# Pairwise bilinear products: output stores of one size and a ring buffer without gaps

## Chip, cores, metric

One core of one Trainium2 chip. The metric is the device time of one execution in microseconds (us).

## The reference, cut to what matters

```python
# inputs: (4096, 32, 64) float32; W: (496, 64, 64) float32, one matrix for each pair of fields i < j
vi = inputs[:, i_idx, :]
vj = inputs[:, j_idx, :]
vdotw = jnp.einsum('bpd,pde->bpe', vi, W)
inter = vdotw * vj
return inter.reshape(B, -1)          # (4096, 31744) float32: 520 MB
```

A little is read (42 MB) and much is written (520 MB). The kernel works in 32 batch tiles of 128 rows; one tile makes 31,744 output columns on each of 128 partitions.

## The kernel before

PE (the matmul engine) multiplies field i (transposed) by its weights into PSUM (its result memory), DVE (the vector engine) multiplies the PSUM result by field j and writes the product into a ring in SBUF (the core's main on-chip memory), and the queue of SyncE stores pieces of the ring. Fields are handled in pairs (2p and 2p+1), whose outputs are `width[2p]` and `width[2p+1]` columns wide.

```python
STORES = [[0, 1], [2, 3], [4, 5], [6, 7, 8], [9, 10, 11, 12, 13, 14, 15]]   # field pairs of a store
RING = 28160
...
    store_w = [sum(width[2 * p] + width[2 * p + 1] for p in g) for g in STORES]
    # 7552, 6528, 5504, 6336, 5824 columns
...
    ring = const.tile([P, RING], F32, tag="ring", name="ring")
    at = 0
...
    for t in range(NT):
        ...                                        # load x of the next tile
        for s, group in enumerate(STORES):
            if at + store_w[s] > RING:
                at = 0                             # the rest of the ring stays empty
            osb = ring[:, at : at + store_w[s]]
            at += store_w[s]
            o0 = off[2 * group[0]]
            for p in group:
                ...                                # transposes for the next tile
                for c0 in range(0, width[2 * p], BANK):
                    ...                            # two matmuls into pm, one for each field
                    if n[0] == n[1]:
                        nc.vector.tensor_tensor(   # both fields in one instruction
                            runs(osb, o[0], o[1], n[0]), pm[:, :, : n[0]],
                            runs(xt, xj[0], xj[1], n[0]), ALU.mult)
                    else:
                        ...                        # one instruction for each field
            nc.sync.dma_start(out=out[ts(t, P), o0 : o0 + store_w[s]], in_=osb)
```

## Time and profile before

| | before |
|---|---|
| time, median | 1341.14 us (1341.14 to 1341.35, 3 runs) |
| span of the profiled run | 1339.7 us |
| PE, DVE, ACT busy | 86%, 88%, 5% |
| DMA queues together, share of 16 engines | 98.8% |
| transfers to the output | 160, 2752 to 3776 KB |

Busy shares of the engines are averages. Here the resource to watch is DMA: 16 engines work in parallel on every transfer, and a transfer counts as landed only when each has done its share: every transfer of this trace ends with 16 semaphore packets. "Share of 16 engines" says how long packets were under way, divided by 16 times the span. The issue lines of the page add how long a store is under way (columns: what, issuer, count, KB, median us from issue to landing), and its queue lines have packets, MB, share:

```profile
out_dram<-ring SPq DMA_DIRECT2D x32, 3776.0 KB, 22.8
...
out_dram<-ring SPq DMA_DIRECT2D x32, 2752.0 KB, 22.1
...
q14 instruction: 23, 0.19, 0.0%
```

The largest and the smallest store take the same 22 us, although a queue at 420 GB/s moves 3776 KB in 9.2 us: each waits behind one or two others. q8 and q14 carry the instructions themselves, fetched in blocks of 16 KiB (q8) and 8 KiB (q14). The main lines follow in the prediction, each with its reading.

### The profile page before, as it was taken

Reading aid. Unit: us, or ns where it says so; the run is one execution under the profiler, and the core shown is the slowest. Engines: PE = TensorE matmul, PEld = TensorE weight load, DVE = VectorE, ACT = ScalarE, POOL = GpSimd, SP = SyncE. Lnnn points to the kernel's source line nnn. Section 1 sums busy time; section 2 is a strip of 40 time slices with the busy share of each in tenths; the row PEclk is TensorE's granted clock in tenths of the full one; section 3 lists DMA queues with packets and bytes.
Section 4 is the critical chain, followed back from the end, with each engine's and each line's share of the span. In section 5 each row is a group of like instructions: output and inputs, shape, how many; then the busy total and the mean of one; then the engine's idle time right before and its main releaser. Section 6 shows DMA issues by size and latency. Waiting matters only on the chain.

```text
span 1339.7 us, 13755 instructions
## 1 busy us (share of the span) xinstructions
PE 1151.0 (86%) x5376; PEld 548.7 (41%) x5376; DVE 1177.4 (88%) x1664; ACT 66.1 (5%) x65; POOL 0.7 (0%) x6
## 2 busy tenths in 40 slices
PE   7998889888898888988888978889798897888992
PEld 3444344443343443443433534444344443444441
DVE  6999889888899988989888989899898997898993
ACT  1000000000000000000000000000000000000000
POOL 0000000000000000000000000000000000000000
PEclk9999889999999999989999899899898998998996
DMA  9999999999999999999999999999999999999996
GB/s 392 426 431 434 429 431 429 427 427 434 426 434 430 422 422 430 422 424 429 415 426 424 426 426 404 415 420 431 428 420 408 431 427 431 416 424 420 422 429 264
DMA packets 30017, 562.93 MB, mean 420 GB/s; under 512 B 3456, under 2 KB 3840, under 8 KB 5376
## 3 DMA queue, kind: packets, MB, share of 16 engines
q1 hardware_dynamic: 25344, 528.49, 92.6%
q10 hardware_dynamic: 4608, 33.56, 6.0%
q8 instruction: 42, 0.69, 0.2%
q14 instruction: 23, 0.19, 0.0%
HBM read 41.94 MB, written 520.09 MB: 420 GB/s over the span
## 4 chain that ended last, share of the span: by engine, by line
DMA 54%; DVE 23%; PE 11%; issue 9%; DVEq 0%
DMA out_dram<-ring 54%; DVE ring L130 15%; PE pm L120 9%; DVE ring L139 9%; PE pt L80 2%; DMA x<-in_x_dram 1%; DVEq L130 0%; DVEq L177 0%
## 5 line engine op out<-in xcount | busy, mean ns | idle before, releaser
L120 PE MATMUL pm<-w,xT 64*128 64x512 f32 (+7 forms) x4864 | 1083.2, 559 | 158.3 <-DVE ring L130 140.1
L130 DVE TENSOR_TENSOR ring<-pm,x 128x1024 f32<-128x1024 f32 x768 | 904.0, 1217 | 138.4 <-DMA out_dram<-ring 93.0
L120 PEld LDWEIGHTS pm<-w,xT 64*128 64x128 f32 x4864 | 487.7, 194 | 720.1 <-DVE ring L130 451.3
L139 DVE TENSOR_TENSOR ring<-pm,x 128x448 f32<-128x448 f32 (+6 forms) x896 | 330.2, 415 | 3.6 <-PE pm L120 2.9
L81 ACT COPY xT<-pt 128x1024 f32<-128x1024 f32 x64 | 64.8, 1012 | 1194.6 <-PE pt L80 1194.6
L80 PE MATMUL pt<-ident,x 128*128 128x128 f32 x512 | 76.5, 297 | 8.5 <-DMA x<-in_x_dram 8.5
L80 PEld LDWEIGHTS pt<-ident,x 128*128 128x128 f32 x512 | 61.0, 152 | 48.9 <-issue 35.3
L81 ACT ACT_TABLE_LOAD x1 | 1.3, 1283 | 1.7 <-PEq L173 1.7
masks.py:199 POOL TENSOR_SCALAR_AFFINE_SELECT ident<-ident 128x128 f32<-128x128 f32 x1 | 0.3, 292 | 0.1
masks.py:197 POOL MEMSET ident<- 128x128 f32 x1 | 0.2, 204 | 0.3 <-POOLq L173 0.3
L173 POOL MEMSET const-bfloat16-1.0<- 128x1 bf16 x1 | 0.1, 101 | 0.0
L173 POOL MEMSET const-uint8-127<- 128x1 uint8 x1 | 0.1, 101 | 0.0
L173 POOL MEMSET const-float32-0.0<- 128x1 f32 x1 | 0.1, 98 | 0.2 <-issue 0.2
L173 POOL MEMSET const-float32-1.0<- 128x1 f32 x1 | 0.1, 98 | 0.0
## 6 DMA issues: line engine op xcount, KB each, us to landing
out_dram<-ring SPq DMA_DIRECT2D x32, 3776.0 KB, 22.8
out_dram<-ring SPq DMA_DIRECT2D x32, 3264.0 KB, 21.8
out_dram<-ring SPq DMA_DIRECT2D x32, 3168.0 KB, 22.4
out_dram<-ring SPq DMA_DIRECT2D x32, 2912.0 KB, 22.3
out_dram<-ring SPq DMA_DIRECT2D x32, 2752.0 KB, 22.1
x<-in_x_dram ACTq DMA_DIRECT2D x32, 1024.0 KB, 14.2
w<-in_w_dram SPq DMA_DIRECT2D x1, 992.0 KB, 7.4
w<-in_w_dram SPq DMA_DIRECT2D x1, 928.0 KB, 11.7
```

The source lines that it names most:

```text
L80: nc.tensor.transpose(pt[:, ts(c, P)], xt[:, ts(n * g + c, P)], ident)
L81: nc.scalar.copy(xT[:, ts(g, 2 * BANK)], pt)
L120: nc.tensor.matmul(pm[:, h, : n[h]], xT[h * D : (h + 1) * D, ts(p, P)], w_sb[p][h * D : (h + 1) * D, c0 : c0 + n[h]], start=True, stop=True,)
L130: nc.vector.tensor_tensor(runs(osb, o[0], o[1], n[0]), pm[:, :, : n[0]], runs(xt, xj[0], xj[1], n[0]), ALU.mult,)
L139: nc.vector.tensor_tensor(osb[:, o[h] : o[h] + n[h]], pm[:, h, : n[h]], xt[:, xj[h] : xj[h] + n[h]], ALU.mult,)
L173: nc = bacc.Bacc("TRN2", target_bir_lowering=False, num_devices=1)
```

## The change

The intent: stores of one size (eight of 3968 columns a tile) instead of five unequal ones, and a ring of exactly seven of them in which nothing stays empty, so that more output is in flight and places come free in smaller pieces. Products are now placed by their output column modulo the ring, without regard to pairs; a product that meets the ring's end is cut.

```diff
-STORES = [[0, 1], [2, 3], [4, 5], [6, 7, 8], [9, 10, 11, 12, 13, 14, 15]]
-RING = 28160
+STORE_W = 3968
+RING = 7 * STORE_W
...
-        for s, group in enumerate(STORES):
-            if at + store_w[s] > RING:
-                at = 0
+        g0 = t * sum(width)
+        sent = 0
+        for p in range(NPR):
...
+                at = [(g0 + o[h]) % RING for h in range(2)]
-                    if n[0] == n[1]:
+                if n[0] == n[1] and at[0] < at[1] <= RING - n[1]:
                     ...                                    # one instruction for both fields
+                else:                                      # pieces, cut at the ring's end
                     for h in range(2):
+                        k = 0
+                        while k < n[h]:
+                            a = (at[h] + k) % RING
+                            m = min(n[h] - k, RING - a)
                             ...
+                            k += m
-            nc.sync.dma_start(out=out[ts(t, P), o0 : o0 + store_w[s]], in_=osb)
+                done = o[0] + n[0] if c0 + n[0] < width[2 * p] else o[1] + n[1]
+                while sent + STORE_W <= done:
+                    a = (g0 + sent) % RING
+                    nc.sync.dma_start(
+                        out=out[ts(t, P), sent : sent + STORE_W], in_=ring[:, a : a + STORE_W])
+                    sent += STORE_W
```

## The prediction

> **What bounds the kernel now.** I read the page's slices and queues first, to see which resource is full.
>
> ```profile
> DMA  9999999999999999999999999999999999999996
> GB/s 392 426 431 434 429 431 429 427 427 434 426 434 430 422 422 430 422 424 429 415 426 424 426 426 404 415 420 431 428 420 408 431 427 431 416 424 420 422 429 264
> ...
> q1 hardware_dynamic: 25344, 528.49, 92.6%
> q10 hardware_dynamic: 4608, 33.56, 6.0%
> q8 instruction: 42, 0.69, 0.2%
> ```
>
> The reader sees 16 DMA engines at 9 tenths or more in 39 of 40 slices; weights and stores (q1), loads of x (q10) and fetched instructions (q8) fill 98.8% of them. PE (86%) and DVE (88%) have room. Only the last slice is low, so I cut the end of the run into stretches (time, PE, weight loads, DVE, ACT, POOL, clock, DMA share, GB/s):
>
> ```profile
> 1233.00:1310.00 77.00, 69.84 (x318) 34.09 (x314) 70.49 (x101) 2.02 (x2) 0.00 (x0) 0.95 1.00 426
> 1310.00:1320.00 10.00, 6.21 (x28) 3.50 (x28) 9.26 (x18) 0.00 (x0) 0.00 (x0) 0.83 0.93 398
> 1320.00:1328.00 8.00, 0.00 (x0) 0.00 (x0) 0.00 (x0) 0.00 (x0) 0.00 (x0) 0.66 0.91 389
> 1328.00:1338.40 10.40, 0.00 (x0) 0.00 (x0) 0.00 (x0) 0.00 (x0) 0.00 (x0) 0.50 0.06 25
> ```
>
> The compute is over before 1320 us. From 1328 to 1338.4 us the share is 0.06, one sixteenth: **one DMA engine works on alone for 10.4 us after the other 15 have finished.** I call it the late engine. The packet records of the trace (start, duration, size) say where the delay comes from. Of the 128 row packets of a tile's first store, the last 8 (one engine's share) end after the other 120 by 1.6 us in tile 0, 2.2 us in tile 2, 6.9 us in tile 10, 10.0 us in tile 18, and then 8 to 11 us to the end. So one engine carries more than the others: every engine has the same rows, and the 42 fetches of 16,384 bytes on q8 are what differs. Which engine carries them the records do not name; that it is this one I infer from the sum below.
>
> From 1328 us to its end its packets follow each other without a gap. Is it ever idle earlier? It ends the first store of tile 2 at 119.4 us, of tile 17 at 736.1, of tile 18 at 777.1, of tile 31 at 1309.6: 41.1 us a tile in the first stretch, 41.0 in the second. It never slows down, although its lag stops growing. What changes is the other 15: from tile 18 on they run dry at times (slices 24, 29 and 30 at 404 to 420 GB/s), because a ring place comes free only when the late engine has read it. The waits of DVE and of the store queue:
>
> ```profile
> DVE ring L130 <- DMA out_dram<-ring: 93.0, 53, 3.3
> DVE ring L130 <- PE pm L120: 45.4, 52, 13.2
> ...
> SPq L145 <- DVE ring L139: 1228.7, 159, 10.5
> ```
>
> DVE waits 93 us in all for the ring, at most 3.3 us at once, while a store takes 22 us from issue to landing: two stores and more are always queued, so the late engine does not starve in these waits. The sum for it, from medians of the records: 8 rows of each of five stores (818+865+940+968+1119 ns) x 32 tiles = 1205.8 us; x, 8 rows x 309 ns x 32 = 79.1; the 16 weight loads 20.6; semaphore writes (9 ns each) 1.9; together 1307.4 us. It runs from about 2.8 to 1338.4 us, 1335.6 us, which leaves 28 us. 42 fetches at 611 ns (16,384 bytes at the line below) are 25.7 us. That nearly closes it. **The time is the late engine's own work from start to end, with about 2.8 us before and 1.3 us behind.**
>
> **What the Trainium skill says.** "DMA: Bandwidth & Descriptors", section "Specifications", gives a ceiling of 435 GB/s for the 16 engines, 27.2 a piece; the records agree, since a byte costs 0.0367 ns (27.2 GB/s). Its section "Why a DMA increments its semaphore by 16 and not by 1" says that each engine adds one and that only the full 16 means all data landed; that is why the slowest engine frees the ring, and the lag that levels off at 10 us agrees. "Runtime: NRT & Kernel Launch", section "Instruction fetch mechanics", says instructions come in blocks of 16 KiB, 256 each, over a DMA queue; PE has 5376 matmuls and 5376 weight loads, 10,752 in all, exactly 42 blocks, which is what q8 shows. "VectorE: DVE Perf Modes", section on the TRN2 errata, gives (N+151)/0.96 ns for a float32 tensor_tensor: 1224 ns for 1024 elements and 224 for 64, where the trace has 1217 and 215.
>
> **The change, part by part.**
> Bytes: stored and loaded bytes are the same. PE's instructions are the same, so q8 stays at 42 fetches.
> Packets: five rows per partition and tile become eight of 15,872 bytes. The medians of the records lie on a straight line, 9.1 ns + 0.03674 ns a byte (22,016: 818; 30,208: 1119; the three between within 1 ns), so a row should take 592 ns. Consecutive packets of one engine overlap in the records by 3 to 4 ns (in the tail, rows of 865 ns start every 861), so a row's real overhead is about 5.2 ns, a semaphore write's 6. Per engine and tile this adds 3x8 = 24 rows and 3 semaphore writes: 24x5.2 + 3x6 = 143 ns, x 32 = **4.6 us, all on the late engine's path**. With the recorded 9 ns uncut it would be 27 x 9 x 32 = 7.8 us. This is the whole direct cost.
> DVE: from the programs' order DVE has 1737 multiplies for 1664, 73 more: pairs cut at the ring's end or whose second row wraps. The shapes' rows give 148 ns fixed (64 columns 215 ns, 448 columns 617), so 73 x 148 = 10.8 us, 0.34 us a tile. DVE goes from 36.8 to 37.1 us busy a tile against 41 for the late engine: beside other work, worth nothing.
> Store issues: 256 for 160 at 0.33 us each on a queue that mostly waits: nothing. The eight DMA semaphores are reused after eight transfers and the ring holds seven stores, so that wait is over before it starts.
> Ring: before, places left empty at the end keep it at four to five stores in flight or being filled. After, it is 27,776 columns always in use and freed in pieces of 3968 (4.7 us of pure row time) rather than up to 7552. DVE's waits for the ring should fall from 93 us to some 40 to 80, and the 15 others should starve less and finish further ahead, the lag growing to perhaps 12 to 18 us. **That gains nothing: they do not set the end.** If anything the late engine loses a little: its 41.0 us a tile with others idle was 41.1 with them busy, about 1 to 2 us over 14 tiles.
> Start: the first store could go about 6 us earlier, but the store queue is still issuing weights up to 23.7 us (its first store left at 24.6), and the DMA share is already 1.0 from 4 us on. Nothing.
> End: a smaller last store shortens the part behind DVE's last write, but the late engine has some 20 us of queued work by then. Nothing.
> Sum: 1341.1 + 4.6 + 1 = about **1347 us**.
>
> **The rivals.**
> *The ring's gaps starve DMA, and filling them gains.* For it: slices at 404 to 420 GB/s and 93 us of DVE waits. If all 16 engines ran at the 430 GB/s of the early stretches, 562.9 MB would take 1309 us, and with start and end some 1315 to 1320, almost 2% less. Against: the lost share belongs to the 15 engines that are ahead; the late engine's pace does not change. A ring moves none of its work. I give it 6%.
> *Smaller packets cost more than the line says*, for instance where x rows or fetches interleave (rows beside x loads show extra time, on average 21 ns for the last store's rows). If every added row cost 25 ns, the sum would be 24x25x32 = 19 us, 1360 us. Against: rows of 6400 to 7424 bytes of the weights lie on the same line, and the extra time is counted twice, in two overlapping packets.
> *DVE becomes the bound, since split writes wait for places further ahead.* It would need 3.5 us more a tile; 0.3 are added. Waiting with five stores queued still leaves some 25 us of DMA work.
> *Rows at whole multiples of 512 bytes are faster* (two of the old stores start or end half-way). The line fits those stores' medians within 1 ns, so I expect nothing.
>
> **Range and chances.** The core of the estimate is 1346 to 1349 us (4.6 to 7.8 us). Packet costs a little worse or a fetch that now overlaps better widen it to 1341 to 1353 us, 8 times in 10. Over 2% faster would need under 1315 us, below what even the first rival makes likely; over 2% slower needs 1368 us, a packet overhead five times what is seen. Same is nearly certain.
>
> **What would show it.** Right: row packets of about 592 ns; q1 with 39,168 packets, 528.5 MB and a share that has hardly moved; q8 still 42; a tail at share 0.06 longer than 10.4 us; DVE's waits for the ring shorter and the middle slices nearer 430 GB/s, with the end no earlier. The late engine's pace should be about 41.2 to 41.3 us a tile. Wrong: a shorter tail with an earlier end (the late engine was held by the ring after all), or rows well above 592 ns.

## The result

| | before | after |
|---|---|---|
| time, median | 1341.24 us (1341.14 to 1341.47, 4 runs) | 1346.80 us (1346.57 to 1346.95, 4 runs) |
| span of the profiled run | 1339.7 us | 1344.9 us |
| DVE: instructions, busy | 1664, 1177.4 us | 1737, 1181.6 us |
| 15 engines finish, last engine finishes (packet records) | 1328.2, 1338.4 us | 1326.1, 1343.7 us |

The ratio is 1.0041 (95% interval 1.0024 to 1.0058), slower by 5.6 us. By the measure of 2% used here the two kernels count as the same; the 5.6 us are small but clear of the noise.

The slices and queues of the kernel after:

```profile
DMA  9999999999999999999999999999999999999994
GB/s 387 429 431 425 425 429 425 425 425 426 430 427 426 425 424 430 425 427 425 425 425 428 427 426 424 424 430 426 424 426 427 425 425 422 424 419 420 426 428 176
...
q1 hardware_dynamic: 39168, 528.50, 92.9%
q10 hardware_dynamic: 4608, 33.56, 5.9%
q8 instruction: 42, 0.69, 0.2%
q14 instruction: 25, 0.20, 0.0%
```

The dips to 404, 408 and 415 GB/s in the middle are gone, and between the first slice and the last none is under 419. A reader who stopped here would expect a faster kernel. But the last slice fell from 264 to 176. Its stretches (time, PE, weight loads, DVE, ACT, POOL, clock, DMA share, GB/s):

```profile
1310.00:1320.00 10.00, 4.06 (x26) 2.25 (x24) 6.84 (x15) 0.00 (x0) 0.00 (x0) 0.97 1.00 423
1320.00:1328.00 8.00, 0.00 (x0) 0.00 (x0) 0.00 (x0) 0.00 (x0) 0.00 (x0) 0.50 0.55 234
1328.00:1338.40 10.40, 0.00 (x0) 0.00 (x0) 0.00 (x0) 0.00 (x0) 0.00 (x0) 0.50 0.06 26
1338.40:1344.00 5.60, 0.00 (x0) 0.00 (x0) 0.00 (x0) 0.00 (x0) 0.00 (x0) 0.50 0.06 26
```

The 15 engines finished 2.0 us earlier than before, at 1326.1 us, and then one engine worked alone for 17.6 us instead of 10.3. What the deeper ring gave to the 15 did not reach the end. The waits of DVE:

```profile
DVE ring L124 <- DMA out_dram<-ring: 106.2, 74, 2.8
...
DVE ring L136 <- DMA out_dram<-ring: 9.8, 12, 2.3
```

Together DVE waits 116 us for ring places, where it waited 93. The landings of the tiles' last stores are 41.2 to 41.3 us apart in most tiles, where they were 41.0 to 41.2 before: the late engine keeps its pace, with a little more work.

### The profile page after: what moved, and what is told of

The parts are those of the page before. It is cut to its first block, busy times and chain, and to the rows that moved or that the text cites. A ratio compares the mean times of both kernels' runs of the same rounds, so it can differ in the third digit from the quotient of the medians.

```text
span 1344.9 us, 14075 instructions
## 1 busy us (share of the span) xinstructions
PE 1138.1 (85%) x5376; PEld 534.3 (40%) x5376; DVE 1181.6 (88%) x1737; ACT 66.1 (5%) x65; POOL 0.7 (0%) x6
## 3 DMA queue, kind: packets, MB, share of 16 engines
q1 hardware_dynamic: 39168, 528.50, 92.9%
q10 hardware_dynamic: 4608, 33.56, 5.9%
## 4 chain that ended last, share of the span: by engine, by line
DMA 66%; DVE 15%; PE 10%; issue 6%; DVEq 0%
DMA out_dram<-ring 66%; DVE ring L124 10%; PE pm L113 8%; DVE ring L136 5%; PE pt L78 2%; DMA x<-in_x_dram 1%; DVEq L124 0%; DVEq L182 0%
## 5 line engine op out<-in xcount | busy, mean ns | idle before, releaser
L124 DVE TENSOR_TENSOR ring<-pm,x 128x1024 f32<-128x1024 f32 x727 | 854.1, 1214 | 124.6 <-DMA out_dram<-ring 106.2
L113 PEld LDWEIGHTS pm<-w,xT 64*128 64x128 f32 x4864 | 477.9, 191 | 738.7 <-DVE ring L124 429.8
L136 DVE TENSOR_TENSOR ring<-pm,x 128x256 f32<-128x256 f32 (+7 forms) x1010 | 379.7, 425 | 10.6 <-DMA out_dram<-ring 9.8
L78 PE MATMUL pt<-ident,x 128*128 128x128 f32 x512 | 71.4, 284 | 8.6 <-DMA x<-in_x_dram 8.6
L78 PEld LDWEIGHTS pt<-ident,x 128*128 128x128 f32 x512 | 56.4, 143 | 42.1 <-issue 39.4
```

Source lines behind the costliest of these rows:

```text
L78: nc.tensor.transpose(pt[:, ts(c, P)], xt[:, ts(n * g + c, P)], ident)
L113: nc.tensor.matmul(pm[:, h, : n[h]], xT[h * D : (h + 1) * D, ts(p, P)], w_sb[p][h * D : (h + 1) * D, c0 : c0 + n[h]], start=True, stop=True,)
L124: nc.vector.tensor_tensor(runs(ring, at[0], at[1], n[0]), pm[:, :, : n[0]], runs(xt, xj[0], xj[1], n[0]), ALU.mult,)
L136: nc.vector.tensor_tensor(ring[:, a : a + m], pm[:, h, k : k + m], xt[:, xj[h] + k : xj[h] + k + m], ALU.mult,)
```

## The experiments

Ten kernels ran, each with five rounds (runs 3, 4 and 6 have four times); the runs of before beside them had medians of 1341.23 (runs 1 to 4), 1341.30 (5 to 8) and 1341.32 us (9 and 10). All results were correct. "Tail" is the time, from the packet records, between the second last engine's end and the last one's.

| run | time, us | against before | ratio, 95% interval | packets q1, blocks q14 and q8 | tail, us |
|---|---|---|---|---|---|
| before | 1341.24 | | | 25,344, 23, 42 | 10.3 |
| after | 1346.80 | +5.6 | 1.0024 to 1.0058 | 39,168, 25, 42 | 17.6 |
| 1 ring only | 1343.40 | +2.2 | 1.0003 to 1.0028 | 29,952, 24, 42 | 10.8 |
| 2 five places | 1346.65 | +5.4 | 1.0028 to 1.0053 | 39,168, 25, 42 | 9.1 |
| 3 sixteen stores | 1361.38 | +20.2 | 1.0134 to 1.0165 | 76,032, 29, 42 | 7.6 |
| 4 split rows | 1394.83 | +53.6 | 1.0385 to 1.0414 | 25,365, 23, 42 | 10.2 |
| 5 more PE code | 1418.46 | +77.2 | 1.0558 to 1.0586 | 25,344, 23, 63 | PE bound |
| 6 more POOL code | 1357.75 | +16.5 | 1.0109 to 1.0137 | 25,344, 63, 42 | 10.3 |
| 7 four stores | 1340.08 | -1.2 | 0.9978 to 1.0003 | 20,736, 21, 42 | 1.9 |
| 8 four places | 1347.11 | +5.8 | 1.0031 to 1.0056 | 39,168, 24, 42 | 4.2 |
| 9 some more PE code | 1346.20 | +4.9 | 1.0024 to 1.0049 | 25,344, 23, 50 | 8.9 |
| 10 three places | 1361.76 | +20.4 | 1.0139 to 1.0167 | 39,168, 25, 42 | 0.5 |

The theory at that time: one DMA engine carries the instruction blocks besides its rows, and its work alone sets the end; the change added packets to it. (That it carries PE's blocks did not hold; see after run 6.) The rivals: the ring's depth or gaps carry time, or the cost came from the ring's order and DVE's cut products.

### Run 1: the ring alone

```diff
 # after.py with the old five stores
-STORE_W = 3968
-RING = 7 * STORE_W
+RING = 27776
+CUTS = [7552, 14080, 19584, 25920, 31744]
...
-                while sent + STORE_W <= done:
+                for cut in CUTS:                     # a store that meets the ring's end
+                    if sent < cut <= done:           # goes out in two transfers
```

> The ring part of the change alone: the five old stores (7552 to 5824 columns), but a ring of 27,776 columns used without gaps; a store that crosses the ring's end goes out in two transfers. Theory (the engine that fetches PE's instructions sets the end; only its packets count): about 36 crossings add 8 rows and one semaphore write each, 48 ns x 36 = 1.7 us, so 1343 us (1341 to 1345) though the 15 other engines starve less and finish earlier, and the late engine's lone tail is longer than 10.4 us, 14 us or more. Rival A (the gaps cost time, the small packets hide the gain): 1335 us or less. Rival B (the new ring order itself costs the 5.6 us, not the packets): 1346 to 1348 us.

Measured: 1343.40 us. The queue's packets show 32 splits and not 36 (29,952 - 25,344 = 4608 = 32 x 9 x 16). The gap-free ring and its 73 additional multiplies thus cost 2.2 us with the old stores: 288 more packets per engine at about 5.5 ns (run 3) are 1.6 us, and its 202 more instructions at some 2.5 ns (see after run 6) 0.5. Rival A (a gain that the packets hide) and rival B (the ring costs it all) both fall. One expectation was missed: the tail grew to 10.8 us only, not 14. Slices of 411 and 413 GB/s show that the 15 engines still ran dry at times; probably the places of large stores come free late, gaps or not.

### Runs 2, 8 and 10: the ring's depth

```diff
-RING = 7 * STORE_W
+RING = 5 * STORE_W      # run 2; 4 in run 8, 3 in run 10
```

> The changed kernel with five ring places of 3968 columns in place of seven. Theory: 15 engines starve more and the late engine's lag is capped at some 5 to 8 us, so the lone tail is shorter than before's 10.4 us and DVE waits much more for the ring, but the late engine still has two to three stores queued (10 to 15 us) and the end does not move: 1345 to 1349 us. Rival (ring depth carries the time): 1360 us or more.

> The changed kernel with four ring places of 3968 columns. It looks for the depth at which the ring begins to matter. Theory: the late engine needs some 9 us from a place's release to the next store in its queue ([...]4.8 us of DVE work for 3968 columns[...]), and with four places it has two stores, 10.3 us, queued: just enough, so between 1347 and 1375 us, with the lag of the late engine down to a few us and DVE's waits for the ring well up. Rival (DVE's waits for the ring are themselves lost time): the rise of DVE's waits over the 119 us with five places appears in full in the time.

> The changed kernel with three ring places of 3968 columns, the depth at which the ring should at last count. With three places the late engine has one store queued, 5.2 us, when it frees a place, and needs about 9 us until the next one arrives: it starves about 4 us per store if DVE does not work ahead, 4 x 256 = 1000 us at worst; with DVE filling part of the next place meanwhile I expect 1400 to 1900 us. Rival (depth never matters): 1347 us.

Measured: 1346.65, 1347.11 and 1361.76 us. Seven, five and four places give the same time within 0.5 us. The middle of the kernel after, then the middle and the end of run 2:

```profile
832.00:1233.00 401.00, 346.80 (x1628) 162.18 (x1626) 357.04 (x521) 20.25 (x20) 0.00 (x0) 0.96 1.01 425
...
832.00:1233.00 401.00, 346.89 (x1624) 163.35 (x1626) 358.08 (x534) 20.24 (x20) 0.00 (x0) 0.95 1.00 419
...
1334.40:1343.60 9.20, 0.00 (x0) 0.00 (x0) 0.00 (x0) 0.00 (x0) 0.00 (x0) 0.50 0.06 26
```

Over the same 401 us of the middle the kernel after moved 425 GB/s. In run 2 it is 419, because the 15 engines starve more, and yet the end is where it was: what they lose in the middle only shortens the tail, 17.6, 9.1 and 4.2 us for seven, five and four places. Two expectations were missed on the way: with five places the tail was to be 5 to 8 us, and with five and four DVE was to wait much more for the ring; it waits 118.8 and 125.7 us, after 116.0 with seven. In run 10 the tail is gone (0.5 us), all engines starve together, and then 15 us are lost. That is the depth at which the ring begins to matter. I had expected 1400 to 1900 us there: the estimate lost up to 4 us for each of 256 stores, and 15 us in all came. Probably DVE works further ahead than it took; this was not tested. DVE's waits for the ring, first run 8 and then run 10:

```profile
DVE ring L124 <- DMA out_dram<-ring: 117.4, 89, 3.1
...
DVE ring L136 <- DMA out_dram<-ring: 8.3, 30, 3.0
```

```profile
DVE ring L124 <- DMA out_dram<-ring: 94.3, 60, 2.9
DVE ring L136 <- DMA out_dram<-ring: 32.8, 19, 7.0
```

125.7 us at 1347.11 us, 127.1 us at 1361.76 us: the sum of these waits does not tell a kernel whose ring is deep enough from one whose ring is not. In these runs the tail does.

### Run 3: sixteen stores

```diff
-STORE_W = 3968
-RING = 7 * STORE_W
+STORE_W = 1984
+RING = 14 * STORE_W
```

> The changed kernel with 16 stores of 1984 columns a tile and 14 ring places (same ring): rows of 7936 bytes. Theory: per engine and tile 64 more rows and 8 more semaphore writes than the changed kernel, 64 x 5.2 + 8 x 6 = 381 ns, x 32 = 12.2 us: 1359 us (1356 to 1363). If the recorded 9 ns a packet were the whole cost: 72 x 9 x 32 = 20.7 us, 1367.5 us. Rival (the packets cost nothing, the ring or the DVE splits made the 5.6 us): 1347 us or below.

Measured: 1361.38 us, within the range. The queues:

```profile
q1 hardware_dynamic: 76032, 528.52, 93.8%
q10 hardware_dynamic: 4608, 33.56, 6.2%
...
q14 instruction: 29, 0.24, 0.0%
```

Same ring, same cut products, same bytes; 99 more packets per engine and tile than before (88 rows and 11 semaphore writes), 6 more blocks on q14 and 860 more instructions in the trace. At 2.5 ns an instruction (see after run 6) the packets cost (20.15 - 2.15) / (99 x 32) = **5.7 ns each**; the interval of the ratio allows 5.0 to 6.3. The kernel after has 320 more instructions and gives (5.56 - 0.80) / (27 x 32) = 5.5 ns. Less the q14 blocks that fall on the late engine (see there; by its pace five more in this run and one more in the kernel after, 0.56 us each), the two give 4.8 and 4.9 ns. Two runs that differ by a factor of 3.7 in added packets agree either way, so the packets and not the ring or the cuts carry the cost.

### Run 4: taking rows from the last engine

```diff
-            nc.sync.dma_start(out=out[ts(t, P), o0 : o0 + store_w[s]], in_=osb)
+            if (t, s) in [(8, 0), (16, 0), (24, 0)]:
+                for a, b in ((0, 120), (120, 128)):
+                    nc.sync.dma_start(
+                        out=out[t * P + a : t * P + b, o0 : o0 + store_w[s]], in_=osb[a:b, :])
+            else:
+                nc.sync.dma_start(out=out[ts(t, P), o0 : o0 + store_w[s]], in_=osb)
```

> The kernel before, but the first store of tiles 8, 16 and 24 goes out as one transfer of 120 partitions and one of 8, so that [...]the last engine gets 24 rows fewer (24 x 1.12 = 26.9 us less) and the first eight get 3 rows more (3.4 us). Theory: if the late engine is number 15, the tail of one lone engine disappears and the time falls to 1317 to 1325 us; if it is one of 8 to 14 nothing moves (1341); if one of 0 to 7 the time rises by 3.4 us to 1344.6. Rival (the ring or the DMA system as a whole bounds the kernel, no single engine): 1341 us or slightly more, with no shift by 3.4 us.

Measured: 1394.83 us, outside every expectation; the test failed as a test. The rate in three places of the run:

```profile
GB/s 396 427 430 429 435 427 427 432 430 426 342 374 393 426 414 428 423 420 435 384 318 363 395 429 398 416 426 425 430 385 318 364 397 433 406 422 427 422 427 271
```

Each of the three split stores makes a trough (342, 318 and 318 GB/s). The packet records show that rows of 30,208 bytes, 1119 ns elsewhere, took over 2000 ns for 50, 82 and 74 of the 128 rows of these stores, often 2349. The late engine's last row of these three stores ends 16.4, 18.1 and 18.3 us later than its usual step of 41.1 us, 53 us in all, which is the whole loss. Perhaps engines get in each other's way. The Trainium skill, "DMA: Bandwidth & Descriptors", section "The descriptor swizzle", states that in a transfer to 128 partitions each engine writes the partitions of one port (here they are read). If the 120 rows went over 15 engines, that order would be broken, which would fit the doubling, but no run shows the ports. The lone tail of 10.2 us is still there. That 120 rows leave out the engine with the highest number, as the expectation takes it, no run shows. If they did, that is not the late one; which it is stays open.

### Runs 5, 9 and 6: the instruction blocks

```diff
 # run 5; run 9 the same under "if c0 == 0:", 16 a tile instead of 40
+                    nc.tensor.matmul(
+                        pm[0:32, 0, 0:1], ident[0:32, 0:32], ident[0:32, 0:1],
+                        start=True, stop=True,
+                    )
 # run 6, scratch is one element
+                    for _ in range(4):
+                        nc.gpsimd.memset(scratch, 0.0)
```

> The kernel before with one tiny extra matmul (32x32 by one column, its result overwritten at once) ahead of each of the 40 matmul groups of a tile: 1280 of them, four instructions each on the chip, so 5120 more instructions for PE to fetch, 20 to 21 more blocks of 16 KiB, while stores, ring and DVE's work stay. Theory (the engine that carries PE's instruction blocks sets the end): 62 to 64 blocks on q8 in place of 42, each 0.61 to 0.67 us on that engine, so +12 to +14 us: 1353 to 1356 us, with PE still below 95% busy. Rival (no single engine matters; 0.33 MB more in 563 MB): +0.8 us at most, 1341 to 1342.5 us.

> The fifth run again with fewer extra matmuls, so that PE does not become the bound: 16 tiny ones a tile (512 in all, 2048 instructions, 8 blocks of 16 KiB). In the fifth run PE was busy 1398 us with 40 a tile (278 us of them the tiny ones), so with 16 it needs about 1231 us and has room. Theory: 50 blocks on q8, 8 more at 0.61 us (bytes alone) to 0.82 us (twice what the POOL run showed for 8 KiB), so +5 to +6.6 us: 1346 to 1348 us. Rival (instruction traffic matters only as bytes among 16 engines, and the POOL run was slowed by something else): 1341 to 1342 us.

> Control to the run before: the same number of extra instructions (5120), but one-element memsets on POOL, which nothing waits for. Theory: if POOL's blocks go over another DMA engine than PE's, that engine gets 20 blocks, fewer than the late one's 42, and the time stays at 1341 to 1342 us; if all instruction queues share one engine, 1353 to 1356 us as well. Rival (any extra instruction traffic costs the same): the same time as the run before.

Run 5 is inconclusive. Its page:

```profile
PE 1397.8 (99%) x7936; PEld 610.8 (43%) x7936; DVE 1233.1 (87%) x1664; ACT 66.1 (5%) x65; POOL 0.7 (0%) x6
...
q8 instruction: 63, 1.03, 0.3%
...
PE 99%; DMA 1%; DVE 0%; issue 0%; DVEq 0%
```

The blocks came as expected (63), but the tiny matmuls made PE the bound (99% of the chain that ended last), so the time says nothing of the blocks. Run 9 repeats it with fewer:

```profile
PE 1223.8 (91%) x6400; PEld 579.6 (43%) x6400; DVE 1181.1 (88%) x1664; ACT 66.1 (5%) x65; POOL 0.7 (0%) x6
...
q8 instruction: 50, 0.82, 0.2%
```

PE has room (91%), a tail of 8.9 us says that the late engine still sets the end, q8 carries 8 blocks more, and the time rises by 4.9 us (3.2 to 6.6 by the interval). That is 0.61 us a block of 16 KiB, or 2.3 ns for each of the 2134 more instructions in the trace. Spread over 16 engines, 0.13 MB would be 0.3 us. Run 6 has no PE work added:

```profile
PE 1153.9 (85%) x5376; PEld 544.1 (40%) x5376; DVE 1177.7 (87%) x1664; ACT 66.1 (5%) x65; POOL 456.3 (34%) x5126
...
q8 instruction: 42, 0.69, 0.2%
q14 instruction: 63, 0.52, 0.1%
```

DVE and PE are as busy as before and nothing waits for the memsets, but 40 more blocks of 8 KiB come over q14 and the time rises by 16.5 us: 0.41 us a block, where bytes alone would be 0.31, or 3.2 ns for each of the 5120 memsets. The expectation left open which of its first two cases holds; the time lies 1.8 us above the range of the second. The late engine itself is slowed, and only while the memsets run: up to 752 us its tiles take 42.0 us, afterwards 41.1 as before. So more instructions, for PE or for POOL, lengthen the work of the engine that sets the end.

**Not by their blocks, though: the packet records contradict that.** In the kernel before, the late engine's rows are, from tile 6 on, the last of each store's 128 to end (the last 7 are taken here, and the first 112 for the others). How much longer such a row takes than the prediction's line, 9.1 ns + 0.03674 ns a byte, depends on how many instructions of the trace end meanwhile (mean ns over the line; 3 and 260 rows over by more than 150 ns are left out):

| instructions that end during the row | 0 | 4 to 6 | 10 to 12 | 16 to 20 |
|---|---|---|---|---|
| rows of the late engine | 1 | 12 | 25 | 43 |
| rows of the others | 1 | 1 | 3 | 1 |

That is 2.4 ns an instruction on this engine and nothing on the others (runs 6 and 9: 2.9 and 2.4 ns). A fetch of q8 lasts 936 ns in the records (median). On the late engine its bytes would add 0.6 us to a store, but the 18 stores without x loads that hold a whole fetch take no longer there than the other stores with as many instructions, and in run 6 the same is true of 22 stores that hold a whole block of q14. In 35 of the 42 fetches the row that is lengthened most meanwhile is a store's, by 369 ns or more, and it is never one of the last 8. So the blocks of PE and of POOL fall on engines that have time, as far as the records can place them. What the late engine does for each instruction the records do not show. Every timed run has a span and a clock from its records, so that it is the recording itself is not ruled out. One kind of block does fall on it: once in 64 stores a store takes 0.54 to 0.58 us longer on this engine, each time beside a block of q14: four times in the kernel after, and three times before, where two show only as tiles of 41.7 and 41.6 us in place of 41.1.

### Run 7: fewer, larger stores

```diff
-STORES = [[0, 1], [2, 3], [4, 5], [6, 7, 8], [9, 10, 11, 12, 13, 14, 15]]
+STORES = [[0, 1], [2, 3], [4, 5, 6], [7, 8, 9, 10, 11, 12, 13, 14, 15]]
```

> The kernel before with four stores a tile (7552, 6528, 7872 and 9792 columns), ring and wrapping rule as before. Theory: 8 rows and one semaphore write fewer per engine and tile, at the 6.4 ns that the first four runs give for one packet 58 ns, x 32 = 1.9 us less: 1339.4 us (1338.5 to 1340.5), faster than both kernels, if three or four places still keep the late engine fed. Rival (coarser pieces starve DMA): 1345 us or more.

Measured: 1340.08 us, within the range, but the interval of the ratio (0.9978 to 1.0003) includes 1, so it is not shown to be faster than before; against the kernel after it is 6.7 us shorter by the medians. 9 packets per tile and 114 instructions fewer should have saved 1.6 + 0.3 = 1.9 us, and 1.2 came. The tail of 1.9 us says where the rest may have gone: with four coarse stores the late engine has almost no lead of queued work, as between four and three places above. This was argued, not tested.

## Why the prediction was right, and where it was not

- **The bound is one engine with more work than the others: right, now shown.** Runs 2 and 8 starve the other 15 without moving the end, and runs 3, 6 and 9 put added packets and instructions into the time.
- **That this engine is late because it carries PE's 42 fetches: wrong.** The records show these beside lengthened rows of other engines, and on the late one 2.4 ns for each instruction instead. What these nanoseconds are stays open.
- **Packets, 4.6 us on that engine: right.** Rows of 15,872 bytes have a median of 592 ns as forecast; the runs give 4.8 to 5.7 ns a packet where the records' spacing gave 5.2 for rows, so 4.2 to 4.8 us for the change. The pace of 41.2 to 41.3 us a tile came too.
- **"1 to 2 us over 14 tiles" of lost pace: the sum held, this term did not.** It rests on a misreading. The 41.0 us of the second stretch include the last tile, 39.1 us, in which no x is loaded; without it both stretches have 41.1. What the runs show in its place is 320 more instructions, 0.8 us at 2.5 ns, and one more of the q14 blocks that fall on the late engine. The step "PE's instructions are the same, so q8 stays at 42" was true and incomplete: the other engines' code grew, 73 multiplies and 96 store issues with their semaphore instructions, and it loads the same engine. That the two terms come out alike is luck.
- **The sum for the late engine, "that nearly closes it": closed by luck.** It put 25.7 us of fetches on this engine that the records do not show there, and counted 1664 packets without their overlap of 3 to 4 ns, some 6 us too much. So some 34 us were to be explained; 13,755 instructions at 2.4 ns are 33 us.
- **DVE's waits for the ring, 40 to 80 us: wrong.** They rose from 93 to 116 us. DVE is ahead of DMA and waits for it in the end, 116 to 127 us in all with three to seven places; it waits more often and for shorter times (74 times on its main line, at most 2.8 us, instead of 53 and 3.3). Runs 8 and 10 show that the sum says nothing of the end.
- **DVE's cut products, 10.8 us beside other work: right in effect, wrong in size.** DVE is busy 4.2 us more, and the durations of its multiplies sum to 5.0 us more (1311.9 after 1306.8): the 73 added ones cost about half of 148 ns each. Why is not shown.
- **The tail longer than 10.4 us, the 15 engines better fed, the end no earlier: right** (17.6 us, no middle slice under 419 GB/s). The rival that the ring's gaps starve DMA saw real starvation, on engines that do not set the end.

## What to carry to other kernels

When DMA is 99% busy, do not ask only how busy it is on average; look at the end of the run for a share of one sixteenth. Here a single engine with extra work decided, and better buffering for the other 15 merely lengthened its tail. In this kernel every packet (about 5 to 5.7 ns per engine) and every instruction (2.3 to 3.2 ns) on that engine's path are paid in full, so few large rows and short code are worth more than a finer ring. Here the ring was deep enough as long as the late engine kept a tail; counting the waits of the engine that fills it did not tell. And a sum that closes proves no cause: 42 fetches fitted the late engine's time, and the records place them elsewhere.

## What the Trainium skill lacked or had wrong

- "Runtime: NRT & Kernel Launch", section "Instruction fetch mechanics", calls the cost of crossing a block "mostly hidden". For PE's blocks the records agree as far as they tell: no fetch that can be placed (35 of 42) lies on the late engine. For the q14 block that comes once in 64 stores they do not: 0.54 to 0.58 us each on the engine that sets the end.
- No page has a cost for each instruction on one DMA engine: 2048 more for PE cost 4.9 us and 5120 more for POOL 16.5 us.
- "CRC Debugging", section "Comparing the Two Runs", names queue 14 for the refill of instructions. POOL's blocks came over q14 here, but PE's over q8, 42 to 63 of them.
- The section of "Runtime: NRT & Kernel Launch" named above gives blocks of 16 KiB. q8 has them (42 for PE's 10,752 instructions), but the packets on q14 are of 8192 bytes; 5120 more POOL instructions made 40 more of them.
- "DMA: Bandwidth & Descriptors", section "Why small descriptors are slow (HBM only)", gives a fixed overhead of about 3 cycles a packet as a matter for small descriptors. Rows of 15.9 and 7.9 KB pay too: about 5 to 5.7 ns a packet, 4.2 to 4.8 us of this kernel's time for eight rows in place of five.
- The same page tells how the number of engines follows from the number of rows, but not what an odd split costs: three transfers of 120 and 8 partitions in place of 128 cost 53.6 us, with rows of 2349 ns in place of 1119.
- No page describes a tail at a DMA share of one sixteenth (10.3 us before, 17.6 after) as the sign of one overloaded engine.
